# Layer 0 of a two-layer image kernel: convolution taps issued behind the projection's second half, a mixing product moved ahead of a norm's sums, and the next q, k begun three attention steps later

## The chip, the cores and the metric

The kernel runs on one core of a Trainium2 chip. A core has TensorE (PE, matmuls, with its weight loads listed apart as PEld), VectorE (DVE), ScalarE (ACT), GpSimd (POOL) and SyncE (SP, which here only issues transfers). Each has its own queue of instructions, and they meet through semaphores. TensorE writes to a small accumulator memory (PSUM) that the other engines read; everything else lies in on-chip memory (SBUF) or in the device's main memory (DRAM). The metric is device time in microseconds (us); the runs shown are of the whole kernel, both layers.

## The reference

The input is eight images of 256 channels and 32 x 32 pixels. Layer 0 treats each image alone:

```python
def _forward(x, ...):
    a = _attention(_ln(x, norm1_w, norm1_b), qkv_w, ..., proj_v)
    x = x + gamma1 * a
    f = _edffn(_ln(x, norm2_w, norm2_b), pi_w, dw_w, fft_p, po_w)
    return x + gamma2 * f
```

`_ln` divides each pixel by the root mean square of its channels. `_attention` makes q, k (4 heads of 32 channels) and v (4 heads of 64) with a 1 x 1 convolution and a folded batch norm, takes a softmax over all 1024 pixels, adds a depthwise 3 x 3 convolution of v, and projects back to 256 channels. `_edffn` widens to 1024 channels, runs a depthwise 3 x 3 convolution over each, multiplies gelu of one half by the other half, goes back to 256 channels and filters each 8 x 8 patch in the frequency domain. Layer 1, a causal attention over 2048 tokens and a mixture of eight expert networks, follows it and isn't touched.

## The kernel before, in words

**Tiling.** An image is held as a tile `t` of 128 partitions by 2 channel groups by 1024 pixels. Matmuls take 512 pixels (a half, `h`) or 256 (a chunk of queries) at a time. Three `t` tiles are in rotation: an image's tile is loaded (`load_x`) only after the image three before it has been stored (`td`). There is room for two one-bank accumulators named "mm" in PSUM, for two wider ones ("s"), and for the attention's sums.

**Stages.** Layer 0 is a loop over i from 0 to 7. In stage i, `main_of(i)` lists TensorE's work as a generator: the attention of image i (`attend`, 17 steps: scores `s`, exponentials `pT` on ScalarE, value products `po`, sums `sums`, and a short closing per chunk with `tps`, `trs`, `rb`), the rest of image i-1 (the second half of its projection, `project(i - 1, (1,))`, matmuls `pp`; its second norm, `norm2`), the last part of image i-2 (`spectrum`: mixing product `pz`, eviction `zf`, transform `pf`, filter `gf`, inverse transform `py`, residual add on `t`; then the store of `t` and the load of image i+1), and the preparation of image i+1 (`queries_keys`, then `stack` and `values`).

**The norms** (`rms_norm`) are a chain over all engines: squares `sq` on ScalarE, sums `ms` on TensorE, an eviction `yr`, a transpose `tpy`, powers on GpSimd (`y`, `a`, `r`), a transpose back `tr`, a spreading product `rbn`, and two multiplies `xn` on VectorE for each half.

**`queries_keys`** has twelve steps: eight for the norm with one gap, and four half-groups of the q, k product (`pq`). ScalarE evicts each into `hi`, VectorE forms the remainder `lo`, and after each group both go to DRAM (`part`). `stack` reads them back in another layout (`qst`, `kst`) once the attention of the stage has ended.

**VectorE's side.** `hidden(i - 1, v_conv(i))` is the second generator: 16 taps of the convolution over v of image i (tiles `o`; two ScalarE instructions begin these tiles), then 64 taps for the widening of image i-1 (tiles `x` and `conv`, with matmuls `ph` and evictions `hpad`, `x` before each group of eight). A tap is one VectorE instruction over 1024 pixels. The `ph` of the first group need the norm's `xn`.

**What sets the order.** `level(main, side, share)` merges both lists. Each time `main` yields, it draws steps from `side` while the estimated VectorE time spent is below `share` of the estimated TensorE time. Nothing is drawn between two instructions that `main` issues without a yield. The engine wrappers (`InOrder`) keep each engine's instructions in the order in which they were issued, which is also why nearly all of them carry line 73 in the profile; they are told apart by their tiles. The residual adds of `project` (`t<-pp`) come after its yields:

```python
for g in range(KC):
    conv1x1(pps[g], projw, g * P, att[b]["o"], hs)
    yield 1.7
for g in range(KC):
    tb = t[b][:, g, hs]
    dve.scalar_tensor_tensor(tb, pps[g], proj_o[:, g : g + 1], tb, ALU.add, ALU.add)
```

For the second half both accumulators `pps[g]` are the two "mm" ones. `weave(main, side, every)` passes through `main` and puts in one step of `side` after every `every` steps. Stage 1 has no spectrum; stage 7 prepares no further image; stages 2 to 6 have all parts.

Of the kernel before, what the change touches and what calls it, by code (L numbers as in the profile page):

```python
# [19 lines left out]
B, C, H, W = 8, 256, 32, 32  # L20
# [85 lines left out]
def conv_attn_hybrid_kernel(  # L106
# [371 lines left out]
    with ExitStack() as l0:  # L478
# [204 lines left out]
        def conv1x1(ps, w, o0, src, hs):  # L683
            for k in range(KC):
                pe.matmul(
                    ps, w[:, k, o0 : o0 + P], src[:, k, hs], start=(k == 0), stop=(k == KC - 1)
                )
# [7 lines left out]
        def qkv_group(b, g, take):  # L695
            for h in range(2):
                hs = slice(h * HALF, (h + 1) * HALF)
                pq = ps_m.tile([P, HALF], F32, tag="mm", name="pq")
                conv1x1(pq, qkvw, g * P, att[b]["xn"], hs)
                take(hs, pq)  # L700
                yield 1.7

        def queries_keys(b):

            att[b] = {"xn": one.tile([P, KC, N], F32, tag="xn", name="xn")}
            yield from rms_norm(b, "n1w", att[b]["xn"], 1)  # L710
            for g in range(2):
                hi = one.tile([P, N], F32R, tag="hi", name="hi")
                lo = one.tile([P, N], F32, tag="lo", name="lo")
                bias = qkv_o[:, g : g + 1]

                def take(hs, pq):
                    act.activation(hi[:, hs], pq, AF.Identity, bias=bias)
                    dve.scalar_tensor_tensor(lo[:, hs], pq, bias, hi[:, hs].bitcast(F32), ALU.add, ALU.subtract)

                yield from qkv_group(b, g, take)  # L720
                parts = att[b][g] = [dram.tile([P, N], F32, tag=f"part{g}{r}", name="part", bufs=2) for r in range(2)]
                for part, src in zip(parts, (hi, lo)):
                    nc.sync.dma_start(part, src.bitcast(F32))

        def stack(b):
            for g in range(2):
                hi, lo = att[b][g]
                name = ("qst", "kst")[g]
                att[b][name] = st = one.tile([P, NH, N], F32R, tag=name, name=name)
                for r in range(4):  # L730
                    src = (hi, lo, hi, lo)[r] if g == 0 else (hi, hi, lo, lo)[r]
                    nc.sync.dma_start(
                        st[r * KD : (r + 1) * KD].bitcast(F32), src.rearrange("(h k) n -> k h n", k=KD)
                    )

        def values(b):


            vT = att[b]["vT"] = one.tile([P, NT, C], F32, tag="vT", name="vT")
            waiting = []  # L740

            def turn(g, h, full):
                tp = ps_m.tile([P, 4, P], F32, tag="mm", name="tpv")
                for j in range(4):
                    pe.transpose(tp[:, j, :], full[:, j * P : (j + 1) * P], ident)
                act.copy(vT[:, 4 * h : 4 * h + 4, g * P : (g + 1) * P], tp)

            for g in range(KC):
                bias = qkv_o[:, 2 + g : 3 + g]
                pq = ps_s.tile([P, 2, HALF], F32, tag="s", name="pq")  # L750
                for h in range(2):
                    hs = slice(h * HALF, (h + 1) * HALF)
                    conv1x1(pq[:, h, :], qkvw, (2 + g) * P, att[b]["xn"], hs)
                for h in range(2):
                    full = one.tile([P, HALF], F32, tag="full", name="vfull", bufs=2)
                    act.activation(full, pq[:, h, :], AF.Identity, bias=bias)
                    pool.tensor_copy(interior(vpad[g], h), rows(full))
                    yield 1.7
                    if waiting:
                        turn(*waiting.pop())  # L760
                        yield 0.5
                    waiting.append((g, h, full))
            turn(*waiting.pop())
            yield 0.5
# [113 lines left out]
        def finish(b):  # L878
            for step in att[b]["rest"]:
                step()  # L880
                yield 0.4

        def project(b, halves):
            for h in halves:
                hs = slice(h * HALF, (h + 1) * HALF)
                if h == 0:
                    both = ps_s.tile([P, KC, HALF], F32, tag="s", name="pp")
                    pps = [both[:, g, :] for g in range(KC)]
                else:
                    pps = [ps_m.tile([P, HALF], F32, tag="mm", name="pp") for _ in range(KC)]  # L890
# [6 lines that stand above are left out]
# [3 lines left out]
        def norm2(b, gaps=3):  # L900
            xn2[b] = one.tile([P, KC, N], F32, tag="xn2", name="xn2")
            yield from rms_norm(b, "n2w", xn2[b], gaps)
            ready2[b] = True
# [120 lines left out]
        def gelu_steps(b):  # L1024
            hid = hid_of[b]
            while hid["gelu"] < ng:
                h1 = hid["h"][hid["gelu"]]
                act.activation(h1, h1, AF.Gelu)
                hid["gelu"] += 1
                gate(b)  # L1030
                yield 0.0
# [69 lines left out]
        def weave(main, side, every, rest=True):  # L1101

            for n, us in enumerate(main):
                yield us
                if n % every == every - 1:
                    step = next(side, None)
                    if step is not None:
                        yield step
            if rest:
                yield from side  # L1110

        def some(steps, n):
            for us in itertools.islice(steps, n):
                yield us

        def none():
            yield from ()

        def later_on(n, steps):
            for _ in range(n):  # L1120
                yield 0.0
            yield from steps

        def main_of(i):

            steps = attend(i)
            if i >= 1:  # L1130
                if i == 1:
                    yield from some(steps, 1)
                    yield from project(i - 1, (1,))
                    yield from weave(norm2(i - 1), steps, 2, rest=False)
                else:
                    mixing, second = spectrum(i - 2), norm2(i - 1, 5)
                    yield from some(second, 1)
                    yield from some(mixing, 1)
                    yield from project(i - 1, (1,))
                    for _ in range(3):  # L1140
                        yield from some(second, 1)
                        yield from some(mixing, 1)
                    yield from weave(second, mixing, 1, rest=False)
                    yield from weave(mixing, steps, 2, rest=False)
            yield from weave(steps, queries_keys(i + 1) if 1 <= i < B - 1 else none(), 1)
            gelus = gelu_steps(i - 1) if i >= 1 else none()
            if i + 1 < B:
                stack(i + 1)
                steps, ends = values(i + 1), finish(i)
                yield from some(gelus, 2)  # L1150
                yield from some(steps, 2)
                yield from gelus
                yield from some(ends, 1)
                yield from project(i, (0,))
                yield from some(steps, 2)
                yield from some(ends, 1)
                yield from some(steps, 1)
                yield from ends
                yield from steps
            else:  # L1160
                yield from weave(project(i, (0,)), weave(finish(i), gelus, 1), 1)
                yield from project(i, (1,))
# [21 lines left out]
        for i in range(B):  # L1184


            if i == 0:
                level(main_of(i), v_conv(i), SHARE[0])
            else:
                level(main_of(i), hidden(i - 1, v_conv(i)), SHARE[i])  # L1190
# [799 lines left out]
```

## Time and profile before

| | us |
|---|---|
| median of 3 runs | 3175.88 |
| lowest and highest run | 3171.82, 3175.91 |
| the profiled execution, its time | 3179.9 |
| the profiled execution, its span | 3178.2 |
| stages 2 to 6 of layer 0, from one `pp` of the second half to the next | 165.3, 169.6, 166.7, 167.2, 165.6 |
| VectorE busy in each of these | 129.8 |
| TensorE busy in each of these | 147.6 to 149.8 |

Times in a timeline are the start in us from the start of the span and the time that a group took, then the engine, the operation, what it wrote and read, and the shape and number. In square brackets stands how long the engine stood idle just before it, and what ended the wait. A wait is put down to the signal that came last. VectorE and ScalarE show an instruction's own time; matmuls overlap, so a busy TensorE isn't one at its peak.

### The profile page before, as it was taken

How to read it: one execution, taken by the hardware profiler on the slowest of the kernel's cores; microseconds unless marked ns; L12 is line 12 of the kernel's file. 1: busy time of each engine (PE TensorE's matmuls, PEld its weight loads, DVE VectorE, ACT ScalarE, POOL GpSimd, SP SyncE). 2: the span in 40 equal slices, each digit the busy share in tenths (PEclk: the TensorE clock that was granted, in tenths of full speed). 3: DMA queues.
4: the chain of work that ended last, by engine and by line, in shares of the span. 5: the costliest groups of instructions: out<-in, count | busy, mean ns of one | idle time of the engine just before them, and what ended most of it. 6: DMA issues, size and time to landing. Idle time of an engine off the chain costs nothing.

```text
span 3178.2 us, 41565 instructions
## 1 busy us (share of the span) xinstructions
PE 2934.5 (92%) x16802; PEld 1943.3 (61%) x16802; DVE 2394.3 (75%) x3014; ACT 1562.0 (49%) x2312; POOL 325.9 (10%) x422
## 2 busy tenths in 40 slices
PE   7988897979797989868999999899999999999998
PEld 4544554545455555545666666677777777777776
DVE  2278786868686879685767665588988888888887
ACT  3455453535354536323333333365666666666664
POOL 1011111111111110011222222100000000000000
PEclk8999998989899989989999999999999999999999
DMA  5203030211203020002433221412112142211210
GB/s 179 54 1 80 28 81 27 67 41 45 62 28 80 28 67 1 25 25 88 154 115 120 106 103 56 194 63 73 67 67 93 53 176 98 85 67 67 100 67 28
DMA packets 63599, 234.86 MB, mean 74 GB/s; under 512 B 5590, under 2 KB 13606, under 8 KB 54566
## 3 DMA queue, kind: packets, MB, share of 16 engines
q1 hardware_dynamic: 63094, 230.54, 21.8%
q8 instruction: 134, 2.20, 0.3%
q0 software_dynamic: 304, 1.57, 0.1%
q14 instruction: 67, 0.55, 0.1%
HBM read 140.61 MB, written 91.49 MB: 73 GB/s over the span
## 4 chain that ended last, share of the span: by engine, by line
PE 79%; DVE 14%; ACT 4%; DMA 2%; issue 1%; POOL 0%; SPq 0%; ACTq 0%; DVEq 0%; POOLq 0%
PE pm L73 12%; PE pa L73 11%; PE q L73 11%; PE po L73 10%; PE s L73 8%; PE ph L73 5%; PE pz L73 3%; PE pq L73 3%; DVE conv L73 3%; PE sums L73 3%; DVE x L73 3%; PE pv L73 2%; PE pk L73 2%; DVE o L73 2%; PE pp L73 2%; DVE zt L73 1%
## 5 line engine op out<-in xcount | busy, mean ns | idle before, releaser
L73 PE MATMUL pa<-ze,w 128*128 128x512 f32 x1488 | 423.2, 393 | 0.0
L73 DVE SCALAR_TENSOR_TENSOR x<-hpad,vec,x 128x1024 f32<-128x1024 f32 x248 | 317.6, 1283 | 117.2 <-ACT x L73 110.3
L73 DVE SCALAR_TENSOR_TENSOR conv<-hpad,vec,conv 128x1024 f32<-128x1024 f32 x256 | 329.5, 1289 | 14.5 <-ACT conv L73 8.0
L73 PEld LDWEIGHTS pa<-ze,w 128*128 128x128 f32 x1488 | 278.2, 188 | 63.3 <-issue 3.1
L73 ACT ACTIVATE h<-pa,bn_o,s1a 128x512 f32<-128x512 f32 x256 | 198.6, 776 | 203.5 <-PE pa L73 203.5
L73 ACT ACTIVATE pT<-s 128x1024 f32<-128x1024 f32 x256 | 247.8, 1024 | 74.2 <-PE s L73 73.9
L73 PE MATMUL po<-pT,vT 128*32 128x256 f32 x4096 | 277.6, 389 | 0.0
L73 PE MATMUL q<-h2p,w 128*128 128x512 f32 x768 | 269.0, 459 | 0.0
L73 DVE SCALAR_TENSOR_TENSOR h<-pa,s1b,h 128x512 f32<-128x512 f32 x256 | 191.2, 747 | 93.9 <-PE pa L73 87.7
L73 PE MATMUL ph<-xn,piw 128*128 128x512 f32 x512 | 240.8, 606 | 13.5 <-ACT x L73 11.3
L73 PE MATMUL pm<-h,w 128*128 128x512 f32 x512 | 241.0, 593 | 0.0
L73 PE MATMUL s<-kk,z 128*128 128x512 f32 x512 | 236.8, 594 | 4.1 <-DVE pr L73 4.1
L73 PE MATMUL q<-z_first,w 128*128 128x512 f32 x768 | 217.1, 391 | 2.7 <-DVE z_first L73 1.7
L73 PE MATMUL pm<-h1p,w 128*128 128x512 f32 x768 | 216.8, 390 | 0.5 <-DVE h1p L73 0.5
L73 DVE SCALAR_TENSOR_TENSOR o<-vpad,pe_w,o 128x1024 f32<-128x1024 f32 x128 | 164.0, 1282 | 54.4 <-ACT o L73 51.3
L73 PEld LDWEIGHTS q<-h2p,w 128*128 128x128 f32 x768 | 144.6, 188 | 83.1 <-issue 59.6
L73 PE MATMUL s<-qst,kst 128*128 128x256 f32 x1024 | 182.6, 322 | 9.4 <-ACT pT L73 7.3
L73 PEld LDWEIGHTS po<-pT,vT 128*32 128x32 f32 x4096 | 122.1, 111 | 88.6 <-issue 10.3
L73 PEld LDWEIGHTS s<-qst,kst 128*128 128x128 f32 x1024 | 141.4, 198 | 53.6 <-issue 37.2
L73 ACT ACTIVATE hpad<-ph,pi_o 128x512 f32<-128x512 f32 x126 | 87.0, 690 | 169.9 <-PE ph L73 157.5
L73 PEld LDWEIGHTS q<-z_first,w 128*128 128x128 f32 x768 | 144.4, 188 | 34.4 <-DVE z_first L73 2.9
L73 PEld LDWEIGHTS ph<-xn,piw 128*128 128x128 f32 x512 | 90.8, 191 | 121.1 <-issue 87.5
(269 smaller groups left out, 5103.9 us busy)
## 6 DMA issues: line engine op xcount, KB each, us to landing
ze<-zd SPq DMA_DIRECT2D x29, 1536.0 KB, 6.4
qst<-part SPq DMA_DIRECT2D x32, 512.0 KB, 7.9
kst<-part SPq DMA_DIRECT2D x32, 512.0 KB, 15.1
te<-ud SPq DMA_DIRECT2D x32, 512.0 KB, 4.1
wd<-parts_w SPq DMA_DIRECT2D x20, 768.0 KB, 3.6
w<-wd SPq DMA_DIRECT2D x20, 768.0 KB, 4.7
zd<-parts SPq DMA_DIRECT2D x14, 1024.0 KB, 3.9
t<-in_x_dram SPq DMA_DIRECT2D x8, 1024.0 KB, 5.0
```

The source lines that it names most:

```text
L73: return self._tc.keep_in_program_order(method(*args, **kwargs))
```

## The change

Three things are altered in `main_of`, and a helper `silent` is added, which runs steps of a generator without passing on their yields; `later_on`, which puts empty steps ahead of a generator, was there.

- For i = 1, the first attention step and the projection's second half run silently, so no step of the VectorE side is drawn before the residual adds or until the norm's first yield.
- For i from 2 on, the norm's first squares, the first mixing product and the projection's second half run silently. Then two pairs follow, a mixing step first and a norm step second, instead of three pairs with the norm step first. The second mixing product thus stands between the projection and the norm's sums, and the first draw from the VectorE side comes after it. From the norm's fourth step on the sequence is as before.
- For i from 1 to 6, `queries_keys(i + 1)` is woven with the attention steps after three empty steps.

No instruction is added or left out.

```diff
+        def silent(steps, n=None):
+            for _ in itertools.islice(steps, n):
+                pass
+
...
                 if i == 1:
-                    yield from some(steps, 1)
-                    yield from project(i - 1, (1,))
+                    silent(steps, 1)
+                    silent(project(i - 1, (1,)))
                     yield from weave(norm2(i - 1), steps, 2, rest=False)
                 else:
                     mixing, second = spectrum(i - 2), norm2(i - 1, 5)
-                    yield from some(second, 1)
-                    yield from some(mixing, 1)
-                    yield from project(i - 1, (1,))
-                    for _ in range(3):
+                    silent(second, 1)
+                    silent(mixing, 1)
+                    silent(project(i - 1, (1,)))
+                    for _ in range(2):
+                        yield from some(mixing, 1)
                         yield from some(second, 1)
-                        yield from some(mixing, 1)
                     yield from weave(second, mixing, 1, rest=False)
                     yield from weave(mixing, steps, 2, rest=False)
-            yield from weave(steps, queries_keys(i + 1) if 1 <= i < B - 1 else none(), 1)
+            yield from weave(steps, later_on(3, queries_keys(i + 1)) if 1 <= i < B - 1 else none(), 1)
```

## The prediction

> **What bounds it now.** I read in this order: the page's busy shares, the list of waits, the timeline around one stage change of layer 0 (a stage is one pass of `main_of(i)`), the table of stretches for a whole stage, and stage 7 as a control. In the page, TensorE is busiest and carries most of the final chain, but layer 0, the part that changes, has gaps in every stage:
>
> ```profile
> span 3178.2 us, 41565 instructions
> PE 2934.5 (92%) x16802; PEld 1943.3 (61%) x16802; DVE 2394.3 (75%) x3014; ACT 1562.0 (49%) x2312; POOL 325.9 (10%) x422
> ...
> PE 79%; DVE 14%; ACT 4%; DMA 2%; issue 1%; POOL 0%; SPq 0%; ACTq 0%; DVEq 0%; POOLq 0%
> ```
>
> The list of waits (total, times, longest) names three that matter here; the second and third come about once per stage:
>
> ```profile
> DVE x L73 <- ACT x L73: 110.3, 23, 14.2
> ...
> PE ms L73 <- DVE t L73: 61.3, 7, 10.1
> ...
> ACT sq L73 <- DMA t<-in_x_dram: 42.0, 6, 9.7
> ```
>
> The timeline at the change from stage 1 to stage 2 shows the wait of ms. TensorE ends the projection's second half (pp) at 313.2, then stands still: five taps (o) are queued on VectorE ahead of the residual adds (t) that empty pp's two accumulators, and ms needs one of these.
>
> ```profile
> 309.58 3.60 PE L73 MATMUL pp<-o,projw 128*128 128x512 f32 x8
> ...
> 314.56 6.57 DVE L73 SCALAR_TENSOR_TENSOR o<-vpad,pe_w,o 128x1024 f32<-128x1024 f32 x5 [6.69 <-ACT o L73]
> ...
> 321.04 1.40 DVE L73 SCALAR_TENSOR_TENSOR t<-pp,proj_o,t 128x512 f32<-128x512 f32 x2
> ...
> 321.93 1.08 PE L73 MATMUL ms<-sq,ones 128*32 128x128 f32 x16 [8.76 <-DVE t L73]
> ...
> 329.97 0.69 DVE L73 TENSOR_TENSOR gf<-pf,filt 128x512 f32<-128x512 f32 x1 [3.69 <-PE pf L73]
> ```
>
> The wait of sq comes 35 us later. The squares (sq) for the next q, k sit in ScalarE's queue right after the first attention step's exponentials, and wait for an input tile whose load could only be issued when the previous output had been stored. Behind them wait the next exponentials and the evictions (hpad, x), hence VectorE's next taps and TensorE:
>
> ```profile
> 346.39 1.19 PE L73 MATMUL s<-qst,kst 128*128 128x256 f32 x8
> ...
> 347.57 0.34 SPq L1097 DMA_DIRECT2D td<-t  x1
> ...
> 351.69 0.40 SPq L488 DMA_DIRECT2D t<-in_x_dram  x1
> ...
> 356.62 1.15 ACT L73 ACTIVATE sq<-t 128x512 f32<-128x512 f32 x2 [7.54 <-DMA t<-in_x_dram]
> ...
> 361.90 2.07 PE L73 MATMUL s<-qst,kst 128*128 128x256 f32 x8
> ...
> 362.12 10.53 DVE L73 SCALAR_TENSOR_TENSOR x<-hpad,vec,x 128x1024 f32<-128x1024 f32 x8 [12.06 <-ACT x L73]
> ```
>
> Stretches of stage 2 (busy PE, PEld, DVE, ACT, POOL; clock; DMA), cut at the waits: TensorE is at 28 of 38, 9 of 14.5, and then 92.5 of 93.9 us. What is saved in the first two moves the third, unless VectorE (82.6 of 93.9) can't follow.
>
> ```profile
> 309.60:347.60 38.00, 28.14 (x149) 20.06 (x147) 27.74 (x33) 8.60 (x13) 4.76 (x7) 0.87 0.00 1
> 347.60:362.10 14.50, 9.04 (x81) 4.76 (x82) 2.42 (x2) 6.96 (x11) 0.00 (x0) 0.94 0.39 146
> 362.10:456.00 93.90, 92.45 (x938) 52.94 (x942) 82.55 (x75) 54.13 (x83) 13.43 (x13) 0.99 0.10 34
> ```
>
> **What the Trainium skill says.** "PSUM — Partial Sum Buffer", section "Engine vs sequencer instructions": ScalarE's and VectorE's queues are strict first in, first out, and matmuls start in program order. The trace agrees: two adds, 1.40 us together, held TensorE for 8.76 us because five taps stood before them. "TensorE: Matmul & The Clock Gate", "What's actually happening": after an idle window of about 3.4 us the clock halves, and a busy one restores it. The trace has the same 16 pz products at 5.36 us straight after the 8.76 us gap and at 3.62 later. "DMA: Bandwidth & Descriptors", "Rules for kernel authors": issue a transfer early, compute, wait late. Here the load takes 4.9 us (7.2 in stage 3) and is waited for at once.
>
> **The change, part by part.** No instruction is added or removed; all changes are of order, which I took from the changed build, engine by engine.
>
> *Projection's second half, stages 2 to 7.* The new order on TensorE is pp, pz (second), ms, pf, ms, tpy, pz; on VectorE t, t, seven taps, gf; on ScalarE zf, o, o, then the second sq pair. The adds run as each pp ends, so ms no longer waits: pp ends 313.2, pz takes 3.5 (16 warm), ms follows at 316.7. But the eviction zf stands before o on ScalarE: 316.7 + 0.6 + 1.25 for the first o puts the first tap at about 318.65 instead of 314.56, and the spectrum's first gf now lies behind seven taps. From the first tap to the last residual add of this section (347.54) VectorE had 33 us. Taken from it are the two adds (1.4) and the waits 3.69 + 0.93 + 0.20 + 0.16 = 5.0; the start is 4.1 later. So VectorE, not TensorE, sets this section now: 6.4 - 4.1 = 2.3 if every wait goes. Chaining the pieces item by item (seven taps of 1.31 to 327.8, gf 328.5, pf, and so on) gives 346.1, a gain of 1.4. I take 2; the 8.76 us is not the prize. The upper bound is 8.8, if VectorE didn't bind. Stage 7 has 4.11 + 0.20 + 0.16 + 0.82 + 0.17 + 0.66 = 6.1 of such waits, so up to 3.4; I take 2.
>
> *q, k three steps later, stages 2 to 6.* The load then lands (issue about 350, +5 to 7) well before its squares, some 18 us after the first scores. Stage 7 prepares no q, k and shows what is left without them:
>
> ```profile
> 1184.36 2.05 PE L73 MATMUL s<-qst,kst 128*128 128x256 f32 x8
> ...
> 1190.98 7.13 PE L73 MATMUL ph<-xn,piw 128*128 128x512 f32 x16
> ...
> 1196.11 3.92 DVE L73 SCALAR_TENSOR_TENSOR x<-hpad,vec,x 128x1024 f32<-128x1024 f32 x3 [10.49 <-ACT x L73]
> ...
> 1197.55 1.51 PE L73 MATMUL s<-qst,kst 128*128 128x256 f32 x8
> ```
>
> From first scores to first tap x: 11.75 there, 15.73 in stage 2, so VectorE gains 4.0. From first scores to the third batch: 13.2 there, with 3.5 us of extra ph in it, so 9.7 against 15.5: TensorE gains 5.8. In stage 2 the next ph half also waits 1.45 us because ms holds one of two accumulators; ms is gone from there. With the section above, TensorE is ahead by 2 + 5.8 + 1.45 = 9.2 and VectorE by 6. VectorE's own waits from 362 to 454 (0.83, 1.59, 1.10, 0.90, 1.27, 0.60, 1.43, 0.61, 1.43: 9.8) can take up the difference, though hardly all of it: I take 8.0 a stage, with ends of 5 (VectorE lags, and holds TensorE through lo, xn and the pads) and 10 (the clock recovers too). Moved with q, k are their norm's matmuls, four half-groups of pq, hi and lo, and four stores. In stages 2 to 6 the build keeps all pq among the attention steps: twelve q, k steps plus three are fifteen, of seventeen. The stores go into SP's queue before the stack's eight transfers, which start at 451; the last store would be issued at about then, adding 3 to 6 us before a tile that is next read some 45 us later. That is hidden; without this cover it would cost those 3 to 6.
>
> *Stage 1.* Here the norm (no mixing) has TensorE wait 7.44 for t, from 160.8 to 168.25. Without it ms, s and the exponentials move up, less the squares that pass ahead: 6.2, and VectorE's later wait for xn (5.07) goes with them. From 203 on VectorE is busy nearly without a gap (51.6 of 52.8), so it keeps the 6.2. But here only eleven attention steps are left, so all four q, k halves end up after the attention with two taps among four lo. VectorE waits there about 1.9 for the second hi and 5 for the store of the first lo (5.6 to land, as at 282.2 in the trace), while 2.6 + 1.1 of its old waits there go: 6.2 - 6.9 + 3.7 = 3.0. I take 2, with ends -4 (a loss) and 5.
>
> *Sum.* 5 x 8.0 + 2 + 2 = 44 us, against the profiled execution's 3179.9 (span 3178.2): 3135.9. The median of the runs is 4.0 lower, 3175.88, so 3131.9. Layer 1 is untouched.
>
> **Rivals.** (a) The whole TensorE wait comes back: 8.8 at each change of stage, 5 x (8.8 + 5.8 + 1.45) + 8.8 + 6.2 = 95, about 3081. For it, 61.3 us in the wait list; against it, the later first tap and gf behind seven taps. 0.08. (b) The moved q, k take back most of the gain of the first steps, by lo, xn and the pads on a VectorE that lags: 2 to 4 a stage, 10 to 22 in all, 3154 to 3166. For it, stage 1's bill; against it, the 9.8 us of waits. 0.12. (c) Slower: what happens in stage 1 happens in each stage: q, k fall behind the attention, uncovered: four pq half-groups of 1.72 plus 5.6 for the store, 12.5, against 9.2 gained: +3.3 x 5, and stage 1's lower end, about 3196. It decides once fewer than fifteen attention steps are left when q, k begin; the build has seventeen. 0.05. (d) The two waits only change their name (TensorE for gf, ScalarE for ph) and nothing moves: 3176. 0.02, as stage 7 shows the steps without the load.
>
> **How the numbers follow.** Forecast 0.73, rivals 0.08, 0.12, 0.05, 0.02. This kernel's measurements tell about 0.2% (6 us) from no change; beyond it, faster has 0.93 (forecast, a, b), within it 0.02 (d), slower 0.05 (c). The forecast's own ends are 5 x 5 - 4 = 21 and 5 x 10 + 5 + 3.4 = 58; with a margin below and the near half of (b) the range is 3110 to 3157.
>
> **What would show it.** Right: ms after pp without a wait on t; ScalarE without a wait for the load; the first tap o about 9 us after pp begins, not 5, then taps almost without a gap to the last t; scores to first x about 11.8; stages 2 to 6 each near 158, not 165 to 170; in stage 1 a new wait of lo for its store. Wrong: gf waiting for pf again, a TensorE gap at pf beyond some 3 us, third-stretch TensorE waits on lo or xn, or a late kst.

## The result, and the profile after

| | before | after |
|---|---|---|
| median, us | 3175.89 | 3136.27 |
| lowest and highest, us | 3171.82, 3178.68 | 3131.31, 3137.65 |
| the profiled execution: time, span | 3179.9, 3178.2 | 3137.65, 3135.9 |

The ratio after/before is 0.9873, 95% interval 0.9856 to 0.9891. The medians lie 39.6 us apart. The forecast of 3132 is 4 us below the measured median, which is within the stated range, and the sign is right. No work was added; TensorE's busy sum rose by 10.3 us. The profiled span is 42.3 us shorter, so what shrank is the time in which TensorE had stood still. The first part of the page of the changed kernel:

```profile
span 3135.9 us, 41559 instructions
PE 2944.8 (94%) x16802; PEld 1951.5 (62%) x16802; DVE 2394.8 (76%) x3014; ACT 1562.0 (50%) x2312; POOL 314.2 (10%) x422
```

The list of waits of the changed kernel (total, times, longest). The wait of ms for t, 61.3 us before, is no longer in it. The wait of sq for its load fell from 42.0 to 1.5, and that of the taps x from 110.3 in 23 to 68.7 in 8. Against that, ms now waits 19.5 for its squares (8.6 before), and trs 6.1 in 2 for GpSimd (3.5 in 3).

```profile
DVE x L73 <- ACT x L73: 68.7, 8, 12.6
...
PE ms L73 <- ACT sq L73: 19.5, 10, 7.0
...
PE trs L73 <- POOL rs L73: 6.1, 2, 4.7
...
ACT sq L73 <- DMA t<-in_x_dram: 1.5, 1, 1.5
```

The timeline of the changed kernel at the change from stage 1 to stage 2, the place that the prediction showed of before:

```profile
310.70 3.89 PE L73 MATMUL pp<-o,projw 128*128 128x512 f32 x8
...
314.63 0.75 DVE L73 SCALAR_TENSOR_TENSOR t<-pp,proj_o,t 128x512 f32<-128x512 f32 x1 [0.97 <-PE pp L73]
...
317.98 0.64 PE L73 MATMUL ms<-sq,ones 128*32 128x128 f32 x16
318.08 0.59 ACT L73 COPY zf<-pz 128x512 f32<-128x512 f32 x1 [6.55 <-PE pz L73]
...
318.56 2.37 ACT L73 ACTIVATE o<-vpad,pe_o,pe_w 128x1024 f32<-128x1024 f32 x2
319.91 9.21 DVE L73 SCALAR_TENSOR_TENSOR o<-vpad,pe_w,o 128x1024 f32<-128x1024 f32 x7 [4.53 <-ACT o L73]
...
329.04 0.68 DVE L73 TENSOR_TENSOR gf<-pf,filt 128x512 f32<-128x512 f32 x1
...
339.39 0.38 PE L73 MATMUL tr<-ident,r 128*8 128x128 f32 x2 [1.91 <-DVE gf L73]
...
342.13 2.08 PE L73 MATMUL py<-idft,gf 128*128 128x128 f32 x8 [0.19 <-DVE gf L73]
...
344.24 0.88 DVE L73 SCALAR_TENSOR_TENSOR t<-py,vec,t 128x256 f32<-128x256 f32 x2 [0.85 <-PE py L73]
...
348.25 0.34 SPq L1097 DMA_DIRECT2D td<-t  x1
...
352.22 0.40 SPq L488 DMA_DIRECT2D t<-in_x_dram  x1
...
358.72 5.25 DVE L73 SCALAR_TENSOR_TENSOR x<-hpad,vec,x 128x1024 f32<-128x1024 f32 x4 [7.98 <-ACT x L73]
```

The second add t begins 0.04 us after pp's last product, and ms follows without a wait. But the first tap comes 9.21 us after pp began (4.98 before): its tile is begun on ScalarE by o, which stands behind the eviction zf, which waits for pz. Near the end of the section TensorE waits 1.91 us for gf, and then py takes 2.08 us, 1.16 before. The load is issued at 352.22, and no squares stand behind it: the first tap x starts 11.76 us after the first scores (346.96), 15.73 before. The stretches of stage 2 of the changed kernel (busy PE, PEld, DVE, ACT, POOL; clock; DMA), cut at the same events, and the whole stage:

```profile
310.90:348.30 37.40, 31.76 (x147) 22.71 (x146) 27.73 (x33) 8.04 (x13) 7.45 (x7) 0.82 0.00 1
348.30:356.90 8.60, 8.14 (x69) 4.58 (x67) 2.40 (x2) 4.98 (x6) 0.00 (x0) 0.97 0.65 246
356.90:450.00 93.10, 92.82 (x959) 52.89 (x961) 82.54 (x75) 56.67 (x88) 8.09 (x13) 1.00 0.08 28
310.90:468.90 158.00, 150.68 (x1242) 90.35 (x1241) 129.58 (x128) 81.98 (x126) 20.68 (x26) 0.96 0.20 54
```

The second stretch gave the most: 14.5 to 8.6 us. In the first, 38.0 became only 37.4, with TensorE busy 31.8 instead of 28.1 on the same work: the wait was turned into slower products (clock 0.82, before 0.87). In the third, TensorE is busy 92.8 of 93.1 (92.5 of 93.9 before), and nothing won ahead was given back. Stages 2 to 6 took 158.1 to 158.9 each.

Where the 42.3 us came from. A stage is counted from the first pp of its second half to that of the next; td is the issue of the store of t, and "section" is pp to td. These are differences of starts in the two traces.

| | before | after | gain | predicted |
|---|---|---|---|---|
| up to stage 1 | 155.4 | 153.7 | 1.7 | 0 |
| stage 1 | 154.2 | 157.0 | -2.8 | 2 |
| sections of stages 2 to 6, mean | 38.20 | 37.85 | 5 x 0.35 = 1.75 | 5 x 2 |
| rest of stages 2 to 6, mean | 128.67 | 120.72 | 5 x 7.95 = 39.75 | 5 x 6 |
| stage 7: section, rest | 41.71, 106.54 | 41.08, 106.98 | 0.2 | 2 |
| after stage 7 | | | 1.7 | 0 |

In stages 2 to 6 the sections, where the order was changed, won nearly nothing; the rest, where q, k were moved, won nearly all.

### The profile page after: what moved, and what is told of

Read it like the earlier page. It is cut to its first block, busy times and chain, and to the rows that moved or that the text cites. A ratio compares the mean times of both kernels' runs of the same rounds, so it can differ in the third digit from the quotient of the medians.

```text
span 3135.9 us, 41559 instructions
## 1 busy us (share of the span) xinstructions
PE 2944.8 (94%) x16802; PEld 1951.5 (62%) x16802; DVE 2394.8 (76%) x3014; ACT 1562.0 (50%) x2312; POOL 314.2 (10%) x422
## 3 DMA queue, kind: packets, MB, share of 16 engines
q0 software_dynamic: 304, 1.57, 0.1%
## 4 chain that ended last, share of the span: by engine, by line
PE 81%; DVE 13%; ACT 3%; issue 1%; DMA 1%; POOL 1%; SPq 0%; ACTq 0%; DVEq 0%; POOLq 0%
PE pm L73 12%; PE pa L73 11%; PE q L73 11%; PE po L73 11%; PE s L73 8%; PE ph L73 6%; DVE o L73 4%; PE sums L73 3%; PE pq L73 3%; PE pz L73 2%; PE pv L73 2%; PE pk L73 2%; DVE conv L73 2%; PE pp L73 2%; DVE x L73 1%
## 5 line engine op out<-in xcount | busy, mean ns | idle before, releaser
L73 DVE SCALAR_TENSOR_TENSOR x<-hpad,vec,x 128x1024 f32<-128x1024 f32 x248 | 316.7, 1283 | 76.2 <-ACT x L73 68.7
L73 DVE SCALAR_TENSOR_TENSOR h<-pa,s1b,h 128x512 f32<-128x512 f32 x256 | 191.5, 748 | 93.9 <-PE pa L73 86.8
L73 PEld LDWEIGHTS pm<-h1p,w 128*128 128x128 f32 x768 | 144.7, 188 | 31.7 <-DVE h1p L73 0.9
```

The lines of the kernel that those rows point to most:

```text
L73: return self._tc.keep_in_program_order(method(*args, **kwargs))
```

## The experiments

Diffs are against the changed kernel where nothing else is said. Each ratio is against the kernel before, run beside it.

| kernel | median, us | ratio (95%) | stage 1 | section | rest |
|---|---|---|---|---|---|
| before | | | 154.2 | 38.20 | 128.67 |
| changed kernel | 3136.27 | 0.9873 (0.9856 to 0.9891) | 157.0 | 37.85 | 120.72 |
| new order alone | 3167.5 | 0.9976 (0.9967 to 0.9985) | 148.2 | 38.08 | 128.32 |
| delay alone | 3140.57 | 0.9889 (0.9874 to 0.9905) | 163.5 | 38.09 | 120.14 |
| delay from stage 2 on | 3130.48 | 0.9857 (0.9842 to 0.9872) | 148.8 | 37.61 | 120.52 |
| taps ahead of the mixing | 3113.13 | 0.9805 (0.9792 to 0.9819) | 157.1 | 33.34 | 120.63 |
| both of these | 3103.86 | 0.9771 (0.9758 to 0.9785) | 148.4 | 33.39 | 120.53 |
| mixing not moved | 3111.71 | 0.9797 (0.9782 to 0.9812) | 157.1 | 33.60 | 120.22 |
| delay of 7 | 3152.77 | 0.9926 (0.9911 to 0.9942) | 157.0 | 36.68 | 124.34 |
| delay of 1 | 3170.01 | 0.9983 (0.9975 to 0.9991) | 157.0 | 37.32 | 126.59 |
| delay of 1, powers two steps later | 3136.74 | 0.9884 (0.9868 to 0.9899) | 157.2 | 36.68 | 120.50 |
| delay of 2 | 3142.99 | 0.9898 (0.9883 to 0.9913) | 156.1 | 38.02 | 121.63 |
| mixing not moved, delay from stage 2 on | 3103.7 | 0.9779 (0.9766 to 0.9792) | 147.8 | 33.84 | 120.22 |
| all three | 3099.91 | 0.9763 (0.9749 to 0.9776) | 148.2 | 33.13 | 120.37 |

The stage, section and rest (means of stages 2 to 6) are each from one profiled execution, in us.

### The two halves alone

The theory: q, k begun later bring the gain, and the new order merely turns one wait into others. The rival: the order brings most. First the order without the delay:

```diff
-            yield from weave(steps, later_on(3, queries_keys(i + 1)) if 1 <= i < B - 1 else none(), 1)
+            yield from weave(steps, queries_keys(i + 1) if 1 <= i < B - 1 else none(), 1)
```

> The new order at the change of stage alone, q and k begun as before. Theory (the load wait carries the gain, the new order is nearly spent on a later start of the taps): stage 1 gains 6, each of stages 2 to 7 gains 0 to 2 between the start of pp and the store of t, the squares still wait 7 to 10 us for the load: 8 to 18 us in all, 3158 to 3168. Rival (the 8.8 us that TensorE stood before ms come back): 8.8 in each of six stages and 6 in stage 1, 59 us, about 3117.

The new order alone took 3167.5, 0.24% less than before. The wait of ms for t is gone, but in stages 2 to 6 almost nothing is won by it. The timeline of this kernel at the change to stage 2:

```profile
302.22 3.60 PE L73 MATMUL pp<-o,projw 128*128 128x512 f32 x8
...
309.20 0.65 PE L73 MATMUL ms<-sq,ones 128*32 128x128 f32 x16
...
311.13 9.21 DVE L73 SCALAR_TENSOR_TENSOR o<-vpad,pe_w,o 128x1024 f32<-128x1024 f32 x7 [4.53 <-ACT o L73]
...
340.61 0.34 SPq L1097 DMA_DIRECT2D td<-t  x1
...
349.70 1.15 ACT L73 ACTIVATE sq<-t 128x512 f32<-128x512 f32 x2 [7.20 <-DMA t<-in_x_dram]
```

The first tap is 8.9 us after pp, the store 38.4 after it (38.0 in stage 2 before), and the squares still wait 7.20 us for the load. What it wins is in stage 1, 6.0 us, and in stage 7's section, 41.71 to 39.95.

Then the delay without the order, which is the kernel before with one line altered (this diff is against it):

```diff
-            yield from weave(steps, queries_keys(i + 1) if 1 <= i < B - 1 else none(), 1)
+            yield from weave(steps, later_on(3, queries_keys(i + 1)) if 1 <= i < B - 1 else none(), 1)
```

> q and k three steps later alone, the order at the change of stage as before. Theory: stages 2 to 6 gain 7 to 8 each from the vanished wait for the load (35 to 40), the wait of ms for t stays at 8 to 10 us; stage 1 loses about 5, as its q and k fall behind the attention and nothing is gained at its start: 30 to 35 us in all, 3141 to 3146. Rival (the order carries the gain): less than 15 us, above 3161.

The delay alone took 3140.57, just under the expected 3141 to 3146: by itself it brings 35 of the 40 us. The list of waits of this kernel shows TensorE's wait for the adds as long as before, to the tenth of a microsecond, beside a load that is no longer waited for:

```profile
PE ms L73 <- DVE t L73: 61.3, 7, 10.1
...
ACT sq L73 <- DMA t<-in_x_dram: 1.8, 1, 1.8
```

Of the 61.3 us, 8.76 lie in each of stages 2 to 6, 7.44 in stage 1 and 10.07 in stage 7. Taken away by this order alone, the 8.76 were worth 0.1 us in a section and 0.35 in the rest of a stage, but the 7.44 in stage 1 were worth 6.0. The wait for the load, taken away by the delay, was worth 8.5 a stage. The delay alone also made stage 1 longer, by 9.3 us. Beside the delay the order won 6.5 in stage 1 and nothing elsewhere: stages 2 to 6 are 0.3 longer on the mean than with the delay alone, and stage 7 is 2.1 longer.

### Stage 1

The timeline of the changed kernel in stage 1, where the q, k steps begin with eleven attention steps left:

```profile
256.51 1.11 POOL L73 TENSOR_TENSOR rs<-sr,rs 128x8 fp32r<-128x8 f32 x1
...
257.67 0.59 PE L73 MATMUL trs<-ident,rs 128*8 128x128 f32 x2 [4.72 <-POOL rs L73]
...
265.79 1.28 DVE L73 SCALAR_TENSOR_TENSOR conv<-hpad,vec,conv 128x1024 f32<-128x1024 f32 x1 [5.59 <-ACT conv L73]
...
284.62 0.75 DVE L73 SCALAR_TENSOR_TENSOR lo<-pq,qkv_o,hi 128x512 f32<-128x512 f32 x1 [2.20 <-ACT hi L73]
...
287.35 1.27 ACT L73 ACTIVATE hi<-pq,qkv_o 128x512 fp32r<-128x512 f32 x2 [2.76 <-DMA part<-hi]
288.65 0.75 DVE L73 SCALAR_TENSOR_TENSOR lo<-pq,qkv_o,hi 128x512 f32<-128x512 f32 x1 [2.08 <-ACT hi L73]
```

Two losses stand here. Two of the lo wait for hi, 2.20 and 2.08 us on VectorE, and before the second of them hi waits 2.76 for the store of part. And the attention's trs waits 4.72 us for rs, which stands on GpSimd behind the norm's powers a, y, y, y, a, r, r, 10.2 us from 246.00; VectorE then waits 5.59 for the evictions conv. The delay was kept for the later stages only:

```diff
-            yield from weave(steps, later_on(3, queries_keys(i + 1)) if 1 <= i < B - 1 else none(), 1)
+            yield from weave(steps, later_on(3 if i > 1 else 0, queries_keys(i + 1)) if 1 <= i < B - 1 else none(), 1)
```

> As the changed kernel, but in stage 1 q and k begin at once as before; the delay holds for stages 2 to 6. Theory: stage 1's early gain of 6 us was given back at its end by four q, k half-groups after the attention (VectorE waits for hi and for the stores); without that, stage 1 is 5 to 8 us shorter than in the changed kernel: 3128 to 3131. Rival (the end of stage 1 is bound by other work): no change, 3136.

It took 3130.48, as the theory had it. Stage 1 fell from 157.0 to 148.8, and these waits are gone: in stage 1 the order wins and the delay loses more. This run removes both losses together; that GpSimd's alone costs so much is tested below for the later stages only.

### The late first tap

If the section's length is set by the first tap, the draw from the side list has to come before the second mixing product, so that ScalarE has o ahead of zf. One empty yield does this; on TensorE, VectorE and GpSimd no instruction of layer 0 changes place.

```diff
                     silent(project(i - 1, (1,)))
+                    yield 0.0
                     for _ in range(2):
```

> As the changed kernel, but for i from 2 on the side list is drawn once between the projection's second half and the second mixing product. TensorE's and VectorE's orders stay as they are; on ScalarE the two instructions that begin the o tiles stand before the second eviction zf instead of behind it. Theory (VectorE sets the section, and its first tap waits for o behind zf behind pz): the first tap comes 3 to 4 us earlier, and each of six stages gains 2 to 3.5: 12 to 20 us, 3116 to 3124. Rival (the norm's chain or TensorE sets the section): the taps start earlier and then wait, below 4 us in all, 3132 to 3137.

3113.13, more than the theory gave it. The timeline of this kernel, change to stage 2:

```profile
312.88 3.61 PE L73 MATMUL pp<-o,projw 128*128 128x512 f32 x8
...
316.53 2.37 ACT L73 ACTIVATE o<-vpad,pe_o,pe_w 128x1024 f32<-128x1024 f32 x2 [2.85 <-PE pp L73]
317.87 9.21 DVE L73 SCALAR_TENSOR_TENSOR o<-vpad,pe_w,o 128x1024 f32<-128x1024 f32 x7 [0.59 <-ACT o L73]
...
346.13 0.34 SPq L1097 DMA_DIRECT2D td<-t  x1
```

The first tap comes 4.99 us after pp instead of 9.21, the store 33.25 after it instead of 37.55: 4.2 us earlier, and 4.3 us earlier. Stages 2 to 6 keep 4.5 each, stage 7's section 4.8 (36.25). VectorE does set the section, and the place of o on ScalarE sets VectorE.

This and the delay from stage 2 on, together:

> The side list drawn before the second mixing product (as in e4) and no delay of q and k in stage 1 (as in e3). Theory (the two lie in different stages and add): 5 to 6 us below e4's 3113, 3107 to 3108. Rival (stage 1's slack is taken up later): 3113.

3103.86, a few us under the expected 3107 to 3108: the two gains add (8.6 us in stage 1, 5 x 4.46 = 22.3 in the sections, 3.9 in stage 7's).

Then the order of the pairs alone put back as it was, the steps ahead of them left silent:

```diff
-                    for _ in range(2):
-                        yield from some(mixing, 1)
+                    for _ in range(3):
                         yield from some(second, 1)
+                        yield from some(mixing, 1)
```

> As the changed kernel, but the pairs of norm and mixing steps keep the old order: ms directly after pp, the second mixing product behind it. Theory (only the start of the taps counts): o no longer stands behind the second zf, only behind the second squares, so the first tap comes about 2 us earlier; gf stands behind one more tap; ms waits under 1 us, since the adds run as each pp ends: 0.5 to 2 us a stage, 3124 to 3133. Rival (the mixing product is needed to cover the adds): ms waits 2 us or more, 3136 to 3150.

A miss in size: 3111.71, 12 us under the theory's best. The change without the moved mixing product is 25 us faster than the change with it. The timeline of this kernel, change to stage 2:

```profile
312.26 3.60 PE L73 MATMUL pp<-o,projw 128*128 128x512 f32 x8
...
318.73 10.53 DVE L73 SCALAR_TENSOR_TENSOR o<-vpad,pe_w,o 128x1024 f32<-128x1024 f32 x8 [2.07 <-ACT o L73]
...
338.34 0.38 PE L73 MATMUL tr<-ident,r 128*8 128x128 f32 x2 [0.71 <-DVE gf L73]
...
341.07 1.16 PE L73 MATMUL py<-idft,gf 128*128 128x128 f32 x8 [0.20 <-DVE gf L73]
...
345.37 0.34 SPq L1097 DMA_DIRECT2D td<-t  x1
```

The first tap comes 6.47 us after pp, 2.7 earlier than in the changed kernel; from it to the store are 26.6 us, there 28.3. The second difference is the one that I hadn't counted. At the end of the section VectorE waits for py and rbn: 0.85 + 0.17 + 0.66 = 1.7 us in the changed kernel, and none of these here, because py takes 1.16 instead of 2.08. 2.7 + 1.7 = 4.4 is what the section of stage 2 fell by. So each of the two edits mends the late tap, and this one the slow products too. It also shows that the new order had two parts of opposite worth: compared with the delay alone, which has the same pairs, the silent steps that put the adds ahead of the taps cut the section from 38.09 to 33.60, and the moved mixing product took nearly all of it back (37.85). With the delay from stage 2 on, it was tried again, and then with the empty yield as well:

> The old order of the pairs (e6) and no delay of q and k in stage 1 (e3). Theory: 6 to 9 us below e6's 3112, 3103 to 3106. Rival (stage 1's gain is taken back): 3112.

> The old order of the pairs (e6), the side list drawn once right after the projection's second half (e4), and no delay of q and k in stage 1 (e3). Theory (e4 and e6 remove one and the same thing, o behind the second zf, so together they give little more than either; e3 adds its own 8): 3099 to 3105. Rival (they add: another 20): 3080 to 3085.

3103.7 and 3099.91, both as expected. The last has the lowest median found, 0.9763 (0.9749 to 0.9776) of before, though its interval overlaps those of the other two at 3104. On top of the pairs put back, the empty yield brings 4 us, not the 23 to 25 that either brings alone: the first tap is then 4.98 us after pp in stage 2, but there TensorE again waits 1.91 at tr, and py takes 2.08.

### How many steps later

Seven empty steps put three of the four q, k half-groups behind the attention in stages 2 to 6, nearly the changed kernel's state in stage 1. This is the mechanism of the slower rival:

```diff
-            yield from weave(steps, later_on(3, queries_keys(i + 1)) if 1 <= i < B - 1 else none(), 1)
+            yield from weave(steps, later_on(7 if i > 1 else 3, queries_keys(i + 1)) if 1 <= i < B - 1 else none(), 1)
```

> As the changed kernel, with seven empty steps instead of three in stages 2 to 6, so that three of the four q, k half-groups fall behind the attention, as in stage 1. Theory (slower by the waits for the stores of hi and lo and for lo, not by the products): 3 to 6 us a stage, 3151 to 3166. Rival (TensorE has the same work and keeps busy): 3136 to 3140.

3152.77: uncovered q, k cost 3.6 us a stage on the rest (0.8 to 7.3), less than half of what the delay brings. The timeline of this kernel at the end of stage 2 has the wait for the store that the prediction had named; it stands in the two stages that lose most, 2 and 6, and in no other:

```profile
454.19 0.75 DVE L73 SCALAR_TENSOR_TENSOR lo<-pq,qkv_o,hi 128x512 f32<-128x512 f32 x1 [4.99 <-DMA part<-lo]
```

One empty step, if all that counts is that the load has landed, should do as well as three (the same line with `later_on(1 if i > 1 else 3, ...)`):

> As the changed kernel, with one empty step instead of three in stages 2 to 6. Theory (only the landing of the load counts, some 10 us after the first scores): the squares wait 0 to 2 us, 3136 to 3144. Rival (the room for accumulators and the first groups of taps need q and k further away): 2 to 4 us a stage given back, 3146 to 3156.

Both expectations missed: 3170.01, nearly all of the gain lost. The load wait is gone (first tap x 11.76 us after the first scores, as in the changed kernel), and the rest of a stage is still only 2 us shorter than before. The timeline of this kernel in stage 2:

```profile
381.78 2.68 POOL L73 TENSOR_TENSOR a<-y,mhalf 128x8 f32<-128x8 f32 x1 [46.36 <-ACT y L73]
...
386.95 1.23 POOL L73 TENSOR_SCALAR y<-y 128x8 f32<-128x8 f32 x1
...
392.36 1.11 POOL L73 TENSOR_TENSOR rs<-sr,rs 128x8 fp32r<-128x8 f32 x1
...
393.52 0.59 PE L73 MATMUL trs<-ident,rs 128*8 128x128 f32 x2 [4.78 <-POOL rs L73]
393.90 4.87 PE L73 MATMUL ph<-xn,piw 128*128 128x512 f32 x8
```

It is stage 1's GpSimd wait, now in every stage: the powers of the norm come just ahead of the chunk's rs, 10.3 us of them, and TensorE waits 4.78 us and then runs ph in 4.87 (3.70 for eight of them in the changed kernel's stage 2). The two together, 4.78 + 1.17 = 5.95, are what the rest is longer by than the changed kernel's, 5.87. The list of waits has 31.4 us in 9 of it, 6.1 in 2 in the changed kernel. To test this, the one step was kept and only the powers were put off, by two empty steps in `rms_norm` ahead of the powers (this diff is against the kernel with one step), so that on GpSimd they come after rs as in the changed kernel:

```diff
+            for _ in range(2 if wname == "n1w" and b > 2 else 0):
+                yield 0.0
```

> As e8 (one empty step), but two empty steps more stand inside the norm of q and k, ahead of its transpose tpy and its powers: squares and sums stay as early as in e8, while GpSimd's order is that of the changed kernel. Theory (e8 lost its time because the norm's powers stand on GpSimd ahead of the softmax's rs, for which TensorE's trs waits 4.8 us a stage): trs no longer waits, 3134 to 3142. Rival (early squares and sums themselves cost it, by accumulators and ScalarE's queue): 3160 to 3172.

3136.74, a ratio of 0.9884 where the changed kernel has 0.9873. The timeline of this kernel in stage 2:

```profile
383.36 1.25 POOL L73 TENSOR_TENSOR rs<-sr,rs 128x8 fp32r<-128x8 f32 x1
386.94 0.38 PE L73 MATMUL trs<-ident,rs 128*8 128x128 f32 x2
...
394.62 0.20 POOL L73 TENSOR_SCALAR y<-y 128x8 f32<-128x8 f32 x1
```

So it isn't the place of the squares and sums, which are as early here as with one step. All that stands behind the powers was put off with them, so this run alone doesn't single the powers out; the sum above and the next run do. With two steps the powers come after rs too, and all else stands only one step ahead of the changed kernel:

> As the changed kernel, with two empty steps instead of three in stages 2 to 6. Theory (only the meeting of the norm's powers with rs on GpSimd makes one step bad; one step later the first rs is through before the powers come): 3134 to 3142. Rival (the gain grows with each step of delay, and one step is a third of three): about 3150 to 3158.

3142.99, 1 us above the theory's end and far from the rival's. Two steps miss the collision: no trs of stages 2 to 6 waits for GpSimd. Their rest is 0.9 us a stage longer than with three. The trace has one new wait for it: in each of these five stages ph waits 1.45 us for an eviction x some 28 us after the store, as it did before the change and doesn't with three steps. The section's 38.02 lies among the changed kernel's own, 37.4 to 38.4.

## Why the prediction was right, and where its steps were not

**The total held on a sum whose terms were off, in part by luck.** Against the 44 us of the sum, the profiled span fell by 42.3 and the median by 39.6; 14.9 us too much for the sections, stage 1 and stage 7 stood against 9.8 too little for q, k and 3.4 outside the change. The step that carried it, q, k three attention steps later, was right in mechanism and too small: the prediction left 6 us a stage for it after what VectorE might take back, and the rest of a stage fell by 7.95 (8.5 with the delay alone). TensorE's 5.8 us ahead was measured as 14.5 - 8.6 = 5.9, and the first tap x after 11.76 is the 11.75 read from stage 7. Two things were mis-sized. VectorE was expected to lag and take back about 1.2, and in the third stretch, where TensorE is busy 92.8 of 93.1, it took back next to nothing: in stage 2 the rest fell by 6.8 of the 7.25 that TensorE was to be ahead by. And stage 2 was read for all five: stages 3 to 5 had longer rests before (128.9 to 130.5, stage 2 127.3), and gained 8.1 to 9.5.

**The projection's second half: the bound was named, its price wasn't.** That VectorE, and not the 8.76 us of TensorE, would set the section was right, and so was the first tap about 9.1 us after pp: 9.21 in stage 2, 8.91 in the others (its pieces, 316.7 + 0.6 + 1.25, give 318.55, or 9.0). The step that failed is "if every wait goes", from first tap to last add: 33 less 6.4 gives 26.6 us, and 28.3 to 29.5 were measured in stages 2 to 6. The gf wait of 3.69 did go; but py in 2.08 us instead of 1.16 put 1.7 us of new waits there, and in stages 4 and 6 gf waits 1.1. The prediction had no term for slower products here. 0.35 a stage came out instead of 2. The run with the pairs put back has the 26.6 in its stage 2. So have five other sections of three kernels that keep the moved mixing product, those in which py took 1.16 (26.5 each, see the end): with the products at that speed the step was right. Stage 7 gave 0.6 in its section and lost 0.4 after it, 0.2 instead of 2.

**Stage 1 was the wrong sign**, within its stated ends (-4 to 5): -2.8 for +2. The 6.2 of the order is there (6.0 in the order alone). The delay was priced at 6.9 less 3.7, 3.2, and cost 9.3 alone and 8.8 beside the order. Of the 6.9, VectorE's waits for hi came (2.20 and 2.08), and the 5 for the store of lo didn't: no lo of stage 1 waits for a store. What is missing is a queue: the prediction listed the norm's matmuls, pq, hi, lo and the stores as what moves with q, k, and not its powers on GpSimd. Their place ahead of rs goes with a wait of 4.72 on TensorE and, behind it, 5.59 on VectorE. VectorE's waits in stage 1 add up to 7.8 more than with the order alone, most of the 8.8.

**What else it had not seen.** Nothing in it says that three is a good number of steps. The run with one shows how near it was: with the powers ahead of rs in each stage it took 3170. That three steps miss it is luck. The up to 3.4 us outside the change (1.7 before stage 1, 1.7 after stage 7) are no part of any step, and lie within what two executions of one kernel differ by.

**The rivals.** The whole TensorE wait (3081) is refuted by the order alone, 3167.5. That the moved q, k take back most (3154 to 3166) didn't happen at three steps; at one nearly all was lost, through GpSimd and not through lo, xn and the pads. The slower rival's mechanism is real but weak: at seven steps, where q, k end behind the attention, the rest of a stage is 3.6 longer than at three and still 4.3 shorter than before; the 12.5 that it was priced at didn't come. No change (3176) is out.

## What to carry to other kernels

Before counting a wait as a gain, ask which engine sets the stretch and what the new order puts ahead of that engine's first instruction: here one eviction ahead of o on ScalarE cost 4 us at each change of stage, and that used up what taking away 8.76 us of TensorE's idle time had won. When a chain is moved, follow it through every queue, the idle-looking ones too: seven tiny operations on an engine that is 10% busy held the busiest one for 4.8 us. Where an edit has two halves, run each alone, and each stage apart: a gain in most stages hid a loss in one, and without that loss and without the moved mixing product the gain was 70 us, not 40.

## What the runs showed of the hardware

**GpSimd beside VectorE's taps.** The same 128x8 operation took 1.23 us in the run with one step, while VectorE ran taps, and 0.20 in the run with the powers put off, in a pause of VectorE (393.7 to 395.1 us). In all 14 traces this operation (`y<-y`) took 1.23 in each of the 92 places where it began during a tap, and 0.20 in the 342 others, among them ten behind which a tap began 0.09 us later. The Trainium skill, "GPSIMD Engine Reference", section "1. Specifications", says that GpSimd shares its SBUF interfaces with VectorE and contends with instructions that have two SBUF inputs, as a tap has. The traces agree, and put it at six times for operations this small, about the length of one tap (1.28).

**TensorE's clock after short waits.** At the end of the section (stages 2 to 7 of all 14 traces, 84 places) tr waits for gf either 1.57 us or more, and then the third py takes 1.83 to 2.08 us in 54 of 59, or 0.71 us or less, and then 1.16 in 22 of 25. "TensorE: Matmul & The Clock Gate", section "What's actually happening", has the clock halve after an idle window of about 3.4 us; here the wait ahead of the slow py was 1.57 to 1.91 us in stages 2 to 6. But this wait doesn't decide it alone. The timeline of the kernel with seven empty steps, stages 3 and 4, has the same instructions, the same wait and both speeds:

```profile
504.45 0.38 PE L73 MATMUL tr<-ident,r 128*8 128x128 f32 x2 [1.91 <-DVE gf L73]
...
507.86 2.08 PE L73 MATMUL py<-idft,gf 128*128 128x128 f32 x8
...
666.18 0.38 PE L73 MATMUL tr<-ident,r 128*8 128x128 f32 x2 [1.91 <-DVE gf L73]
...
668.92 1.16 PE L73 MATMUL py<-idft,gf 128*128 128x128 f32 x8 [0.19 <-DVE gf L73]
```

The granted clock was 0.50 around the first of these py and 1.00 around the second, and the sections took 37.9 and 35.4 us. Five places are like the second: stages 4 and 5 of this kernel, 4 and 6 of the one with the powers two steps later, and 3 of "both of these". In all 14 traces the granted clock is 1.0 or 0.5, and its changes lie whole multiples of 3.41 us apart. What decides whether it changes at the end of a section isn't shown.
